# A convolution, attention and expert kernel: norms, roots and routing of its last part by other operations, in a written-out order

## The chip, the cores and the metric

The kernel runs on one core of a Trainium2 chip, as one launch. Its time is device time in microseconds (us), the median of several runs. A core has five engines that run side by side, each with its own queue of instructions in a fixed order: TensorE (PE in the profile, with its weight loads as PEld), VectorE (DVE), ScalarE (ACT), GpSimd (POOL) and SyncE (SP), which issues most transfers. Engines wait for each other by semaphores. TensorE writes its results to PSUM, a small memory of eight banks; the other data lie in SBUF.

## The reference

The input x has 32 images of 128 channels and 64 x 64 pixels, all float32. Layer 0 is a convolution in a butterfly-transformed domain; layer 1 is attention over the channels and a layer of eight experts of which each token takes two. A token is a pixel with its 128 channels.

```python
def reference(x, ...):
    # layer 0
    x = x + _L0_conv_ref(_gn(x), L0_conv_weight, kd1, kd2, k11, k12, k21, k22)
    # layer 1, on tokens: (32, 4096, 128)
    t = _to_tokens(x)
    t = t + _L1_attn_ref(_ln_t(t), Wk, bk, Wv, bv)
    t = t + _L1_ffn_ref(_ln_t(t), router_w, router_b, expert_w, expert_b)
    return _from_tokens(t, x)

def _ln_t(v, eps=1e-5):
    m = jnp.mean(v, axis=-1, keepdims=True)
    s = jnp.var(v, axis=-1, keepdims=True)
    return (v - m) / jnp.sqrt(s + eps)

def _L1_ffn_ref(x, router_w, router_b, expert_w, expert_b):
    router_probs = jax.nn.softmax(x @ router_w + router_b, axis=-1)
    top_p, top_i = jax.lax.top_k(router_probs, 2)
    top_p = top_p / jnp.sum(top_p, axis=-1, keepdims=True)
    expert_out = jnp.einsum('bnd,edc->bnec', x, expert_w) + expert_b
    gathered = jnp.take_along_axis(expert_out, top_i[..., None], axis=2)
    return jnp.einsum('bnk,bnkc->bnc', top_p, gathered)
```

The attention forms keys and values of each image's normed tokens, multiplies them into a 128 x 128 matrix over all 4096 tokens, takes the softmax of its rows, and applies it to every token.

## The kernel before

The kernel has three parts. The first (until about 927 us) normalizes each image and transforms it forward; the second (until about 2536 us) multiplies by the transformed weights, one column of pixels after another; the last transforms back and does the whole of layer 1. The change lies in the last part alone.

The last part works image by image, with three or four images in flight. An image's tokens lie in `tk` as 32 tiles of 128 tokens x 128 channels. Its steps, with the names that the order uses for them:

- `r0` to `r7` load the image's data of the second part, `x` loads the image itself (2 MB).
- `w0` to `w7` transform back along one axis on TensorE (tile `pu`, L903) into the one buffer `cv`, and `wo` copies it out on ScalarE (L913). `h0` to `h3` transform along the other axis (tile `py`, L925), and `ho` adds the result to the image on VectorE (L933).
- `pt0` to `pt7` turn channels into tokens on TensorE (L1049), `to` copies them to `tk` (L1054), `sa` gathers norm statistics with bn_stats on VectorE (L1021).
- `va`, `pwa` and `na` make mean and inverse root of the first norm: six small operations on VectorE (L1031 to L1036), a power of -0.5 on GpSimd (L1041), two more on VectorE (L1078, L1079).
- `xg` norms four tiles at a time on ScalarE (L1089), `pg` adds their Gram matrix up (L1100), and `gs`, `pb`, `t1`, `pb2`, `sm`, `pr`, `sr`, `sn`, `pc`, `prx` turn it into the attention matrix in `prx`, a tile that also holds the router's weights.
- `pp0`, `pp3` to `pp30` multiply three tiles of tokens each by `prx` (L1173); `at` scales the product on ScalarE (L1186) and copies the router's part to `lq` (L1190); `ad` adds it to `tk` and gathers the statistics of the second norm (L1201, L1021).
- `vb`, `pwb`, `lg`, `nb` make the second norm and the logits; `l2` to `f4`, `f5` and `gt` find the two best experts of each token and their weights, on arrays of 128 x 256 (L1246 to L1276).
- `xn` norms the tokens (L1301), `px` and `xT` turn them (L1311, L1317), `pe` multiplies a tile by four experts (64 an image, L1324), `m` weighs the result on VectorE (L1335), `s` sums the eight experts of a pair of tiles on GpSimd (L1360, L1361, L1363; 16 an image), `st` turns tokens back to channels (tile `po`, L1370), `so` copies and stores them (L1376).

For the last image five of the sixteen pairs are weighed and added on VectorE in one step (L1347) and skip GpSimd.

PSUM's eight banks are shared out as three for `pe`, two for the one buffer `cv`, and three for all the transposes and products (`tl`: `pt`, `pg`, `pb`, `pc`, `pp`, `px`, `po`).

A planner sets the order. Each step is entered with its engine, an estimated length, a due time, the steps it follows, and the buffers that it takes and frees; the due time is the image's number times a slot of 114 us, with a shift for each kind of step. The planner plays the program through once with these lengths, gives each engine the due step that comes first among those that can start, and emits the instructions in the order so found. `prepare` (step `prep`, 3.5 us in the plan) folds the means over the channels into the expert, key and value weights; it comes after `h3` of the first image.

The lines on which the roots and the first sums rest:

```python
nc.vector.tensor_add(total, even[:, :, 1], odd[:, :, 1])
...
nc.vector.scalar_tensor_tensor(var, diff, 0.25, var, ALU.mult, ALU.add)
...
nc.gpsimd.tensor_tensor(rstd, var, mhalf, ALU.pow)
...
nc.vector.scalar_tensor_tensor(nmr, total, -0.5, rstd, ALU.mult, ALU.mult)
```

Of the kernel before, what the change touches and what calls it, by code (L numbers as in the profile page):

```python
# [16 lines left out]
P = 128  # L17
# [3 lines left out]
NE = 8  # L21
# [3 lines left out]
class Plan:  # L25
# [12 lines left out]
    def run(self):  # L38
# [46 lines left out]
        self.length = now  # L85
        for i in order:
            ops[i][3]()
# [3 lines left out]
def kernel(  # L91
# [702 lines left out]
    tps = pool("tps", 3, space=PSUM)  # L794
# [26 lines left out]
    rws = kc.tile([P, NE], F32, name="rws")  # L821
# [7 lines left out]
    def prepare():  # L829
# [21 lines left out]
        nc.vector.tensor_scalar_mul(rws, pe[:, 0:NE], float(P))  # L851

    plan = Plan({"cv": 1, "pe": 3, "tl": 3, "r": 10, "x": 2, "xg": NG, "xn": 2, "xT": 2, "tm": 2, "so": 2, "gate": 2})
    SLOT = 114.0

    SHIFT = {
        "ad": -0.15, "at": -0.25, "f": 0.71, "gs": -1.97, "gt": 0.71, "h": -0.24, "ho": -3.5, "kvp": 3.43,
        "kvq": -0.45, "l": 0.71, "lg": 3.61, "m": -0.32, "na": -1.87, "nb": -0.81, "pb": -1.97, "pc": -1.97,
        "pe": 0.16, "pg": -0.08, "pp": 0.19, "pr": -1.97, "prx": -1.97, "pt": -0.23, "pwa": -1.87, "pwb": 3.61,
        "px": 0.15, "r": -0.04, "s": 0.08, "sa": 1.29, "sm": -1.97, "sn": -1.97, "so": 2.13, "sr": -1.97,  # L860
        "st": 1.1, "t": -1.97, "to": 0.06, "va": -1.87, "vb": 3.61, "w": 0.28, "x": -0.68, "xT": -0.68,
        "xg": 0.21, "xn": 2.42,
    }
    made = {}

    def add(b, key, engine, us, at, run, after=(), take=(), free=(), late=0.0):


        names = [k if isinstance(k, tuple) else (b, k) for k in after]
        at += SHIFT.get(key.rstrip("0123456789_"), 0.0)  # L870
        made[b, key] = plan.add(
            engine, us, SLOT * at, run, [made[k] for k in names if k[0] >= 0], take, free, late
        )


    def transfers(b):
# [4 lines left out]
        def load_r(e):  # L881
            def run():
                i = 8 * b + e
                ring, tag = (rp, "r") if i % 10 < 8 else (rp2, "r2")
                t = rs[b, e] = ring.tile([P, 16 * n], F32, tag=tag, name=f"r{b}_{e}")
                for r in range(2):
                    nc.sync.dma_start(t[r * n : (r + 1) * n], pfv[b, e, r])
            return run
# [6 lines left out]
        add(b, "x", "SP", 0.1, b + 0.2, load_x if b else (lambda: None), take=("x",), late=12.0 if b else 0.0)  # L895

    def conv(b):
        def w_inverse(e):

            def run():  # L900
                ps = tile_of["cv", b, e] = cps.tile([P, 8, P], F32, tag="cv", name=f"pu{b}_{e}")
                for k in range(8):
# [3 lines left out]
                    )  # L906
            return run
# [31 lines left out]
        def w_inverse_piece(e, oh):  # L939

            def run():
                ps = tile_of["cw", b, e, oh] = eps.tile([P, 8, n], F32, tag="pe", name=f"pw{b}_{e}_{oh}")
                for k in range(8):
                    lo = (2 * k + oh) * n
                    for r in range(2):
                        nc.tensor.matmul(
                            ps[r * n : (r + 1) * n, k, :], rs[b, e][:, lo : lo + n], qw[:, r, :], start=True, stop=True
                        )
            return run
# [28 lines left out]
        if b < 2:  # L978
            for e in range(8):
                at = b + 0.08 * e  # L980
                for oh in range(2):
                    add(
                        b, f"w{e}_{oh}", "PE", 0.95, at + 0.04 * oh, w_inverse_piece(e, oh),
                        [f"r{e}"] + [(b - 1, f"h{k}") for k in range(4)], ("pe",), ("r",) if oh else (),
# [13 lines left out]
            if b == 0:  # L998
                add(b, "prep", "PE", 3.5, 0.98, prepare, ["h3"], ("pe",), ("pe",))
# [14 lines left out]
    def front(b):  # L1014
# [4 lines left out]
        def bn(bs, lo, hi):  # L1019
            for i in range(lo, hi):  # L1020
                nc.vector.bn_stats(bs[:, i].rearrange("p a s -> p (a s)"), t[:, i, :])  # L1021

        def moments(which):

            bs = v["bs"]
            even, odd = bs[:, :, 0, :], bs[:, :, 1, :]
            m2 = st.tile([P, 6, NT], F32, name=f"m2{which}_{b}", tag=f"m2{which}", bufs=2)
            total, diff, var, nmr, rstd, above = (m2[:, k, :] for k in range(6))
            if which == 1:
                v["above"] = above  # L1030
            nc.vector.tensor_add(total, even[:, :, 1], odd[:, :, 1])  # L1031
            nc.vector.tensor_sub(diff, even[:, :, 1], odd[:, :, 1])
            nc.vector.tensor_add(var, even[:, :, 2], odd[:, :, 2])
            nc.vector.tensor_mul(diff, diff, diff)
            nc.vector.tensor_scalar(var, var, 1.0 / P, LN_EPS, ALU.mult, ALU.add)
            nc.vector.scalar_tensor_tensor(var, diff, 0.25, var, ALU.mult, ALU.add)  # L1036
            v[which] = total, var, nmr, rstd

        def power(which):
            total, var, nmr, rstd = v[which]  # L1040
            nc.gpsimd.tensor_tensor(rstd, var, mhalf, ALU.pow)  # L1041
# [17 lines left out]
        def stats1(g):  # L1059
            def run():  # L1060
                if g == 0:
                    v["bs"] = st.tile([P, NT, 2, 3], F32, name=f"bs1_{b}", tag="bs", bufs=2)
                bn(v["bs"], 4 * g, 4 * g + 4)
# [9 lines left out]
        add(b, "va", "DVE", 1.7, s1 + 0.14, lambda: moments(1), [f"sa{g}" for g in range(8)])  # L1073
        add(b, "pwa", "POOL", 5.5, s1 + 0.14, lambda: power(1), ["va"])

        def nmr1():
            total, var, nmr, rstd = v[1]
            nc.vector.scalar_tensor_tensor(nmr, total, -0.5, rstd, ALU.mult, ALU.mult)  # L1078
            nc.vector.tensor_scalar_add(v["above"], nmr, 1.0)  # L1079

        add(b, "na", "DVE", 0.9, s1 + 0.14, nmr1, ["pwa"])


        def norm(g):
            def run():
                total, var, nmr, rstd = v[1]
                for k in range(4):
                    i = 4 * g + k
                    nc.scalar.activation(  # L1089
                        xg[g % NG][:, k, :], t[:, i, :], AF.Identity, bias=v["above"][:, i : i + 1], scale=rstd[:, i : i + 1]  # L1090
# [65 lines left out]
        add(b, "pb", "PE", 0.35, at, kv1, ["gs"], ("tl",))  # L1156
# [21 lines left out]
        def scaled(lo, m):  # L1178
            def run():
                total, var, nmr, rstd = v[1]  # L1180
                ps = tile_of["pp", b, lo]
                if lo == 0:
                    v["lq"] = st.tile([P, NT, 2, NE], F32, name=f"lq{b}", tag="lq")
                for k in range(m):
# [4 lines left out]
                    )  # L1189
                nc.scalar.copy(  # L1190
                    v["lq"][:, lo : lo + m].rearrange("p k r e -> p k (r e)"),
                    ps[:, 0 : m * QX].rearrange("p (k q) -> p k q", q=QX)[:, :, P:QX],
# [3 lines left out]
        def added(lo, m):  # L1196
            def run():
                if lo == 0:
                    v["bs"] = st.tile([P, NT, 2, 3], F32, name=f"bs2_{b}", tag="bs", bufs=2)
                ps = tile_of.pop(("pp", b, lo))[:, 0 : m * QX].rearrange("p (k q) -> p k q", q=QX)  # L1200
                nc.vector.tensor_tensor(t[:, lo : lo + m, :], ps[:, :, 0:P], t[:, lo : lo + m, :], ALU.add)  # L1201
                bn(v["bs"], lo, lo + m)
            return run

        for j, lo in enumerate(range(0, NT, 3)):
            m = min(3, NT - lo)
            at = s1 + 0.45 + 0.016 * j
            add(b, f"pp{lo}", "PE", 0.26 * m, at, product(lo, m), ["prx", (b - 1, "lg")], ("tl",), ("x",) if lo == 30 else ())
# [6 lines left out]
                [f"at{lo}"] + (["ad0"] if lo else [f"pg{g}" for g in range(8)]), (), ("tl",),  # L1215
# [12 lines left out]
        def logits1():  # L1228
            total, var, nmr, rstd = v[1]
            lg, eq, lq = row("lg"), row("eq"), v["lq"]  # L1230
            v["lg"], v["eq"] = lg, eq
            nc.vector.scalar_tensor_tensor(nmr, v[2][0], -0.5, nmr, ALU.mult, ALU.add)
            nc.vector.tensor_tensor(lg, lq[:, :, 0, :], by_expert(rstd), ALU.mult)
            nc.vector.tensor_add(lg, lg, lq[:, :, 1, :])
            nc.vector.tensor_tensor(eq, by_expert(nmr), by_token(rws), ALU.mult)
            nc.vector.tensor_add(lg, lg, eq)

        def nmr2():
            total, var, nmr, rstd = v[2]
            nc.vector.scalar_tensor_tensor(nmr, total, -0.5, rstd, ALU.mult, ALU.mult)  # L1240
            nc.vector.tensor_scalar_add(nmr, nmr, 1.0)
            tile_of["norm", b] = rstd, nmr

        def first_max(k):
            m, f, oh = v["tops"][:, 2 * k, :], v["tops"][:, 2 * k + 1, :], v["oh"][k]
# [223 lines left out]
```

## Time and profile before

| what | value |
| --- | --- |
| median of 3 runs | 6045.02 us (6044.08 to 6048.14) |
| the profiled execution | 6034.45 us, its span 6032.7 us |
| granted TensorE clock over the span | 0.994 |
| last part | from about 2536 us to the end |
| one image in the middle of the last part | 106.37 us |

The profile is that of one execution. It gives each instruction's engine, line, tile and duration; a group row gives the number of such instructions, their summed time on the engine, the mean length of one in ns, and how long the engine stood idle just before them and what ended that. Instructions of one engine that overlap are counted once in the busy time, so a row's busy time can be below the mean times the count. Two rows of the last part on engines other than TensorE, as examples:

```profile
L1041 POOL TENSOR_TENSOR m<-m,mhalf 128x32 f32<-128x32 f32 x63 | 342.9, 5442 | 102.7 <-DVE m L1036 102.7
L1248 DVE TENSOR_TENSOR eq<-eq,rank 128x256 f32<-128x256 f32 x64 | 84.8, 1325 | 2.2
```

The first is the power of both norms, two an image; the second one of the steps of the top-2 search.

### The profile page before, as it was taken

What the parts mean: (1) busy time and instruction counts of PE and PEld (TensorE: products, weight loads), DVE (VectorE), ACT (ScalarE), POOL (GpSimd) and SP (SyncE); (2) the same over time, 40 slices, a digit from 0 to 9 for tenths busy, and PEclk for the clock granted to TensorE, in tenths of its full rate; (3) what the DMA queues carried; (4) which work ended last, traced back from release to release, by engine and by line L of the source; (5) the groups of instructions that cost most, each with busy time, mean ns of one, the idle gap of its engine ahead of it and who ended that gap; (6) DMA issues with size and microseconds to landing.
All of it is one profiled execution on the core that took longest, in us unless ns stands there. A gap on an engine that the chain in (4) does not pass through costs nothing.

```text
span 6032.7 us, 219314 instructions
## 1 busy us (share of the span) xinstructions
PE 5884.8 (98%) x95372; PEld 4672.1 (77%) x95372; DVE 4220.6 (70%) x7696; ACT 3757.1 (62%) x7057; POOL 4205.9 (70%) x3793
## 2 busy tenths in 40 slices
PE   7999999999999999989999999999999999999998
PEld 7999999999999999866666666666666666666654
DVE  5565545555555555458778787887878788787888
ACT  7666664555555555467766676676767666676663
POOL 2110006666666666538898998989899888998988
PEclk9999999999999999999999999999999999999999
DMA  5767766666666666632222122221322222132100
GB/s 198 240 226 236 236 217 192 174 172 173 171 173 173 171 173 172 171 102 88 81 71 98 57 98 71 83 86 57 106 63 91 78 74 95 57 100 70 66 27 28
DMA packets 554068, 756.74 MB, mean 125 GB/s; under 512 B 58320, under 2 KB 318928, under 8 KB 549008
## 3 DMA queue, kind: packets, MB, share of 16 engines
q1 hardware_dynamic: 550496, 733.64, 40.3%
q8 instruction: 749, 12.27, 0.9%
q0 software_dynamic: 2608, 9.06, 0.5%
q14 instruction: 215, 1.76, 0.1%
HBM read 406.79 MB, written 335.54 MB: 123 GB/s over the span
## 4 chain that ended last, share of the span: by engine, by line
PE 88%; ACT 7%; issue 2%; DVE 1%; POOL 1%; DMA 1%; SPq 0%; POOLq 0%; ACTq 0%; DVEq 0%
PE pe L1324 28%; PE m L658 17%; PE g L636 9%; PE pf L418 7%; PE pu L903 6%; PE pp L1173 4%; PE py L925 4%; PE pg L1100 4%; PE pv L396 3%; PE px L1311 2%; ACT xn L1301 2%; ACT u L913 2%; PE pz L373 1%; ACT z L383 1%; PE pt L1049 1%
## 5 line engine op out<-in xcount | busy, mean ns | idle before, releaser
L1324 PE MATMUL pe<-ew_sb,xT 128*128 128x512 f32 x4096 | 1946.1, 597 | 19.4 <-DVE tm L1335 16.0
L1335 DVE TENSOR_TENSOR tm<-pe,oh 128x512 f32<-128x512 f32 x2028 | 1346.4, 684 | 479.3 <-PE pe L1324 455.5
L1360 POOL TENSOR_TENSOR tm<-tm 128x512 f32<-128x512 f32 x1014 | 1286.1, 1284 | 201.1 <-DVE tm L1335 182.7
L1324 PEld LDWEIGHTS pe<-ew_sb,xT 128*128 128x128 f32 x4096 | 700.9, 191 | 522.9 <-issue 396.1
L647 DVE COPY f<-g 128x1024 f32<-128x1024 f32 x508 | 622.2, 1225 | 648.9 <-PE g L636 648.9
L658 PE MATMUL m<-f,s 128*64 128x64 f32 x32768 | 1070.1, 224 | 1.9 <-issue 1.1
L658 PEld LDWEIGHTS m<-f,s 128*64 128x64 f32 x32768 | 1000.0, 138 | 63.2 <-issue 2.6
L604 POOL COPY s<-l 128x512 f32<-128x512 f32 x512 | 546.0, 1099 | 524.9 <-issue 508.3
L647 ACT COPY f<-g 128x1024 f32<-128x1024 f32 x508 | 514.5, 1013 | 561.0 <-PE g L636 534.8
L1363 POOL TENSOR_TENSOR tk<-tk,tm 128x256 f32<-128x256 f32 x1014 | 753.6, 743 | 79.5
L1361 POOL TENSOR_TENSOR tm<-tm 128x512 f32<-128x512 f32 x507 | 650.4, 1283 | 39.8
L913 ACT COPY u<-pu 64x512 f32<-64x512 f32 x960 | 556.6, 580 | 135.1 <-PE pu L903 121.5
L636 PE MATMUL g<-c,wst 9*128 9x128 f32 x16256 | 599.9, 283 | 3.6 <-issue 3.3
L636 PEld LDWEIGHTS g<-c,wst 9*128 9x128 f32 x16256 | 502.8, 186 | 38.5 <-issue 3.9
L349 POOL TENSOR_TENSOR grstd<-gms,mhalf 128x1 f32<-128x1 f32 x32 | 17.8, 555 | 735.8 <-DVE gms L345 735.8
L1186 ACT ACTIVATE pp<-pp,m 128x128 f32<-128x128 f32 x1024 | 440.9, 431 | 124.1 <-PE pp L1173 99.3
L606 POOL TENSOR_SCALAR s<-l 128x512 f32<-128x512 f32 x256 | 509.5, 1990 | 0.0
L903 PEld LDWEIGHTS pu<-qw,r 128*128 128x128 f32 x3840 | 455.7, 193 | 63.3 <-ACT u L913 49.5
L903 PE MATMUL pu<-qw,r 128*128 128x128 f32 x3840 | 476.3, 278 | 25.6 <-ACT u L913 25.6
L1317 ACT COPY xT<-px 128x512 f32<-128x512 f32 x256 | 150.2, 587 | 560.5 <-PE px L1311 557.5
L418 PE MATMUL pf<-ph,v 128*128 128x128 f32 x4096 | 491.0, 278 | 5.0 <-ACT z L383 1.1
L418 PEld LDWEIGHTS pf<-ph,v 128*128 128x128 f32 x4096 | 466.9, 192 | 14.7 <-ACT z L383 7.1
(177 smaller groups left out, 8573.0 us busy)
## 6 DMA issues: line engine op xcount, KB each, us to landing
xf<-f SPq DMA_DIRECT2D x512, 256.0 KB
pf<-o SPq DMA_DIRECT2D x1016, 128.0 KB
l<-xf SPq DMA_DIRECT2D x1012, 128.0 KB
r<-pf SPq DMA_DIRECT2D x496, 256.0 KB
x<-in_x_dram SPq DMA_DIRECT2D x256, 256.0 KB
out_dram<-so SPq DMA_DIRECT2D x256, 256.0 KB
y<-in_x_dram SPq DMA_DIRECT2D x31, 2048.0 KB
r<-pf POOLq DMA_DIRECT2D x16, 248.0 KB, 7.7
```

The source lines that it names most:

```text
L418: nc.tensor.matmul(pl[:, j * P : (j + 1) * P], vs[b][:, 8 * g + j, :], ph.rearrange("h r m -> h (r m)"), start=True, stop=True,)
L604: nc.gpsimd.tensor_copy(dst, src)
L636: nc.tensor.matmul(pg[g // 2][:, g % 2, m * P : (m + 1) * P], wst[rows, 16 * half + 4 * t + m, :], c[rows].rearrange("r h k -> r (h k)"), ...
L647: copy(f.rearrange("i m (g o) -> i m g o", g=2), tile_of["g", w, half, t][k].rearrange("i g (o m) -> i m g o", o=4))
L658: nc.tensor.matmul(ps[hh * n : (hh + 1) * n, q, :], s[:, h].rearrange("i k b -> i (k b)")[:, B * r : B * r + n], f[:, h, r, :], start=(r = ...
L903: nc.tensor.matmul(ps[:, k, :], rs[b, e][:, k * P : (k + 1) * P], qw.rearrange("w r m -> w (r m)"), start=True, stop=True,)
L913: nc.scalar.copy(u[r * n : (r + 1) * n, :, oh * n + 8 * e : oh * n + 8 * e + 8], ps[oh * n : (oh + 1) * n, :, r * n : (r + 1) * n].rearran ...
L1324: nc.tensor.matmul(ps, tile_of["xT", b, i // 4][:, i % 4, :], ew_sb[:, es, :].rearrange("d e c -> d (e c)"), start=True, stop=True,)
L1335: nc.vector.tensor_tensor(tile_of["tm", b, i // 2][:, i % 2, es, :], tile_of.pop(("pe", b, i, half)).rearrange("p (e c) -> p e c", c=P), t ...
L1360: nc.gpsimd.tensor_tensor(tm[:, k, 0:4, :], tm[:, k, 0:4, :], tm[:, k, 4:8, :], ALU.add)
L1361: nc.gpsimd.tensor_tensor(tm[:, :, 0:2, :], tm[:, :, 0:2, :], tm[:, :, 2:4, :], ALU.add)
L1363: nc.gpsimd.tensor_tensor(t[:, lo : lo + 2, :], t[:, lo : lo + 2, :], tm[:, :, m, :], ALU.add)
```

## The change

Seven things are changed, all in the last part.

1. bn_stats is followed by bn_aggr for each tile, which gives mean and variance; the six small operations on VectorE are gone.
2. The inverse root is an exponential of a logarithm on ScalarE (`power`), followed by a Newton step on GpSimd (`newton`), where the shifts are made too.
3. The router's weights are centred once, in `prepare`; the logits are built in PSUM while the product is still there, one small VectorE operation a tile, and only half of `lq` is copied.
4. The arrays `lg` and `eq` of the top-2 search lie in PSUM (tile `sc`), so that every step of it has at most one operand in SBUF. One addition moves to ScalarE.
5. For that, the transposes and products have two PSUM banks instead of three.
6. The store is a step of its own (`os`) on SyncE, and the buffers of the loads are taken in the order in which they were freed.
7. The planner no longer finds the order. `follow` emits the steps in a list written out for one image's length: each entry names a step and the stage, so that `pe8_0:4` at turn p is that of image p - 4. The first two and the last two images have small offsets for each kind of step. `prepare` comes beside `pwa` of the first image.

```diff
-    tps = pool("tps", 3, space=PSUM)
+    tps = pool("tps", 2, space=PSUM)
+    sc = pool("sps", 1, space=PSUM).tile([P, 2, NT, NE], F32, name="sc")
...
-        nc.vector.tensor_scalar_mul(rws, pe[:, 0:NE], float(P))
+        for t in prx:
+            nc.vector.tensor_tensor(t[:, P + NE : QX], t[:, P + NE : QX], pe[:, 0:NE], ALU.subtract)
...
+        def bn(which, lo, hi):
+            bs = st.tile([P, 4, 6], F32, name=f"bs{which}_{b}_{lo}", tag="bs", bufs=2)
             for i in range(lo, hi):
-                nc.vector.bn_stats(bs[:, i].rearrange("p a s -> p (a s)"), t[:, i, :])
+                nc.vector.bn_stats(bs[:, i - lo, :], t[:, i, :])
+            for i in range(lo, hi):
+                nc.vector.bn_aggr(v["mv", which][:, i, :], bs[:, i - lo, :])
...
+        def power(which):
+            w = v[which] = st.tile([P, 5, NT], F32, name=f"ln{which}_{b}", tag=f"ln{which}", bufs=2)
+            nc.scalar.activation(w[:, 0, :], v["mv", which][:, :, 1], AF.Ln, bias=epsc)
+            nc.scalar.activation(w[:, 0, :], w[:, 0, :], AF.Exp, scale=-0.5)
+
+        def newton(which):
+
+            mv = v["mv", which]
+            rstd, nmr, above, var, q = (v[which][:, k, :] for k in range(5))
+            nc.gpsimd.tensor_scalar_add(var, mv[:, :, 1], LN_EPS)
+            nc.gpsimd.tensor_tensor(q, var, rstd, ALU.mult)
+            nc.gpsimd.tensor_tensor(q, q, rstd, ALU.mult)
+            nc.gpsimd.tensor_scalar(q, q, -0.5, 1.5, ALU.mult, ALU.add)
+            nc.gpsimd.tensor_tensor(rstd, rstd, q, ALU.mult)
+            nc.gpsimd.tensor_tensor(nmr, mv[:, :, 0], rstd, ALU.mult)
+            nc.gpsimd.tensor_scalar(above, nmr, -1.0, 1.0, ALU.mult, ALU.add)
             if which == 1:
...
+                nc.gpsimd.tensor_scalar_mul(nmr, nmr, -1.0)
...
                 nc.vector.tensor_tensor(t[:, lo : lo + m, :], ps[:, :, 0:P], t[:, lo : lo + m, :], ALU.add)
-                bn(v["bs"], lo, lo + m)
+                for k in range(m):
+                    nc.vector.scalar_tensor_tensor(
+                        sc[:, 0, lo + k, :], ps[:, k, P : P + NE], v[1][:, 0, lo + k : lo + k + 1], v["lq", lo][:, k],
+                        ALU.mult, ALU.add,
+                    )
+                bn(2, lo, lo + m)
...
+            nc.vector.tensor_copy(first, v["tops"][:, 0, :])
+            nc.vector.tensor_tensor(v["tops"][:, 5, :], v["tops"][:, 2, :], first, ALU.subtract)
...
             nc.scalar.activation(g2, g2, AF.Exp)
+            nc.scalar.activation(g1, g2, AF.Copy, bias=1.0)
...
-            nc.vector.tensor_scalar_add(g1, g2, 1.0)
...
-    plan.run()
+    ORDER = """
+        na:3 xn5:4 xT3:4 pe8_0:4 pe9_0:4 m8_0:4 s3:4 xg0:3 m9_0:4 m8_1:4 st0:4 h1:2 xg1:3 pe9_1:4 so0:4 xg2:3 os0:4
...
+        xn7:4 s7:4 pc:3 pe16_0:4 r6:1 prx:3 xT5:4 pe16_1:4 m16_0:4 m17_1:4 pp0:3 m16_1:4 pe17_0:4 at0:3 r1:0 pp6:3
+        m17_0:4 h2:2 at6:3 ad0:3 s8:4 r4:1 ad6:3 pe18_1:4 pp9:3 ho2:2 pe19_1:4 r7:0 at9:3 pe18_0:4 st3:4 m18_0:4
+        h3:2 so3:4 m18_1:4 os1:4 ad9:3 pp3:3 ho3:2 pe19_0:4 at3:3 pp12:3 m19_0:4 pe23_1:4 m19_1:4 at12:3 ad3:3 s9:4
+        w0:1 ad12:3 pe22_0:4 r3:0 wo0_0:1 pp24:3 m22_0:4 pe22_1:4 at24:3 m23_1:4 px6:4 m22_1:4 pe20_0:4 xT6:4 ad24:3
+        pe23_0:4 wo0_1:1 pp30:3 m23_0:4 pe20_1:4 at30:3 m20_0:4 s11:4 pp21:3 ad30:3 w1:1 at21:3 m20_1:4 pp15:3
+        ad21:3 r5:0 wo1_0:1 pe21_1:4 at15:3 pe21_0:4 pe26_0:4 m21_0:4 os3:4 wo1_1:1 m21_1:4 pp18:3 ad15:3 s10:4
+        pe27_1:4 at18:3 w2:1 m26_0:4 ad18:3 pp27:3 wo2_0:1 pe26_1:4 x:1 m27_1:4 at27:3 pe27_0:4 m26_1:4 px7:4
+        m27_0:4 wo2_1:1 pe25_1:4 ad27:3 s13:4 pe24_1:4 xT7:4 pe24_0:4 pwb:3 w3:1 m24_0:4 m25_1:4 m24_1:4 pt1:2
+        pe30_0:4 to1:2 wo3_0:1 pe25_0:4 nb:3 m30_0:4 pt0:2 m25_0:4 st4:4 to0:2 pe30_1:4 s12:4 l2:3 wo3_1:1 pe31_1:4
...
+    """
...
+    plan.follow(list(dict.fromkeys(i for at, i in sorted(turns))))
```

## What the change should do to the time

> **What bounds the kernel now.** I read the page's rows of busy time and clock first, then the granted clock and busy time of one image's length in the last part, then TensorE's waits, then VectorE's rows in order of time.
>
> ```profile
> span 6032.7 us, 219314 instructions
> PE 5884.8 (98%) x95372; PEld 4672.1 (77%) x95372; DVE 4220.6 (70%) x7696; ACT 3757.1 (62%) x7057; POOL 4205.9 (70%) x3793
> ...
> PEclk9999999999999999999999999999999999999999
> ```
>
> TensorE is busy nearly throughout, at a clock that is hardly held back. The change touches only the last part, from about 2536 us on. There the kernel repeats itself: the copy of the Gram matrix (L1113) starts at 5040.77 and again at 5147.14, so one image takes 106.37 us. A stretch of that length, with the columns window, PE, PEld, DVE, ACT, POOL, clock, DMA share, GB/s:
>
> ```profile
> 4000.00:4106.00 106.00, 104.65 (x743) 71.61 (x742) 85.14 (x189) 72.87 (x167) 94.91 (x83) 1.00 0.24 80
> ```
>
> TensorE is idle 1.35% of the time, 1.43 us an image; VectorE, ScalarE and GpSimd all have room. TensorE's waits from 3000 to 5500 us (total, times, longest) say where:
>
> ```profile
> PE pt L1049 <- ACT tk L1054: 18.2, 23, 0.8
> PE pu L903 <- ACT u L913: 12.3, 23, 0.5
> ```
>
> Two places, both behind ScalarE. So in the middle some 28 images hold 28 x 1.43 = 40 us to win, however much work leaves VectorE and GpSimd. The rest lies at the ends: by busy time in stretches of 20 us, TensorE idles 28 of the 220 us from 2540 on and 34 of the last 272.
>
> **The change part by part.** Durations are those of the profiled execution.
>
> *GpSimd.* Two powers leave, each L1041 at 5.44 us. Two Newton sequences of 8 and 7 short operations come; the nearest rows are 128x1 at 0.22 (L353) and 128x64 at 0.34 (L618), so 0.22 to 0.29 each, about 3.8 us. Net 7 us an image less on an engine 95 us busy of 106. In the middle this is worth nothing: TensorE does not wait for it there.
>
> *VectorE, removed.* Moments (L1031 to L1036) 3.6, L1078/1079 0.9, L1232 to L1236 1.9, L1240/1241 1.4, L1272 1.1: 8.9 us an image. The top-2 steps cost 12.0 now because some stretch (L1248 means 1.33, while L1236 of the same shape takes 0.44); at 0.42 each the sixteen take 6.7, 5.3 less.
>
> *VectorE, added.* Aggregations, 64 an image, and 32 scalar-times-tensor steps of 128x8 that build the logits in PSUM. For the latter, L1347 (128x128) takes 350 ns and L339 (128x1) 220, so 0.225; the second and third of a group write the same tile and wait for the one before, as L1247 waits for L1246 and starts 0.04 after its end: 8 us an image. The aggregation has one row only:
>
> ```profile
> L328 DVE BATCH_NORM_AGGREGATE gmv<-gbs x32: 371/372/374, 13.9 to 840.1; 128x2 f32<-128x48 f32 x32
> ```
>
> It reads 16 triples, the new one 2. If the 0.217 us above a shortest operation (0.155) goes by triples, two take 0.03, and behind others an operation hides about 0.085 (bn_stats: 0.28 alone, 0.195 in a row). That is 0.10. Below, 0.08 is the step of short operations less their elements; above, 0.29 is the row itself less the overlap. I take 0.10, since the row's length is most simply explained by what it reads, and keep both ends. VectorE's ledger: 85.1 - 8.9 - 5.3 + 0.2 + 8.0 + 6.4 = 85.5. No relief in sum, and it is bunched: the new work sits in the pieces that free the PSUM buffers of the products. In these rows of now (start, length) a piece is an addition and three bn_stats, done 1.26 us after it began:
>
> ```profile
> 5053.37 0.56 DVE L1201 TENSOR_TENSOR tk<-pp,tk 128x384 f32<-128x384 f32 x1
> 5053.96 0.68 DVE L1021 BATCH_NORM_STATS2 bs<-tk 128x6 f32<-128x128 f32 x3
> 5054.63 1.22 DVE L933 TENSOR_TENSOR y<-py,y 128x1024 f32<-128x1024 f32 x1
> ```
>
> After: 0.49 (addition) + 0.225 + 2 x 0.26 - 0.085 + 3 x 0.195 + 3 x 0.10 = 2.03 us.
>
> *The new order and two transposing buffers instead of three.* I add up the tightest stretch, pp0 to pp30. TensorE does 6 products (0.74), 10 expert products (0.86), 2 h-inverses (2.02), one w-inverse (1.78) and 2 groups of transposes (0.44): 19.7; all of an image's operations so added give 103.6 against 104.9 busy, so 20.0. pp30 takes the buffer that ad24 frees. VectorE reaches ad0 2.5 us in (0.74, a wait of 0.17, ScalarE's 1.57) and does 6 pieces, 2 additions of h (1.14) and 7 weighings (0.60): 6 x 2.03 + 2.28 + 4.2 = 18.7. It ends at 21.3, 1.3 us too late. In general the stall is 18 x a - 0.5, with a the aggregation: 0.9 at 0.08, 1.3 at 0.10, 4.7 at 0.29. Other places in the image are earlier than that by the same sums, so one stall of 1.3 takes the place of 1.43 idle: 0.15 us an image won, 28 x 0.15 = 4 us. While the Gram matrix holds one of the two buffers, st1 and px4 share the other, 3.5 us apart at some 1.2 us of use: no stall.
>
> *ScalarE.* Root and inverse become logarithm and exponential. The page has one row for a table load, ACT_TABLE_LOAD at 1.283 us; the built program has 128 more of them, four an image: each logarithm and each exponential has its own. The Trainium skill (ScalarE: Activation LUTs, What ACT_TABLE_LOAD costs) counts 2.66 us for every switch, the load and a drain; and its section on table sets says that logarithm and exponential share a set, which would need one load where the program has two. By the row, a power is 2 x 1.283 + 2 x 0.23 = 3.0 us; by the page's price, 5.8. ScalarE goes from 73 to 79, or to 84.5. The power waits for the last product piece; queued behind it are the copies to1 and wo3, for which TensorE's st4 (buffer) and w4 wait, and on GpSimd the Newton steps nb and na stand before the sums s12 and s3. In the same frame the last piece ends at 36.2, the power at 39.3 by the row, to1 at 39.9; st4 is due at 40.7. Cover 0.7 us. By the page it is 2.0 late. I take the row, which is this chip's own; whether a drain follows, its trace cannot show, since ScalarE waits for the norm after that load. 5.8 stays as the far end.
>
> *SP.* Loads of r and x and stores stand in one fixed line now, a store waiting for ScalarE before later loads. r2 is issued 33 us before its use and took 7.7 us where the page times it; x (2 MB, at 170 GB/s about 12 us) 41 us before. Nothing, unless a store is held 25 us.
>
> *The head.* On the first image's chain moments, power and shift (1.8 + 5.44 + 0.9) become 3.0 + 2.0: 3 us. prepare (3 us of TensorE and a wait of 2.3 for VectorE behind it) moves beside that chain. I count 5 of the 28 us.
>
> *The tail.* Here GpSimd counts: it is busy 243 of the last 272 us. After the last product TensorE now has 88 expert products; in the built new order 78. Pairs for GpSimd go from 17 to 14.5 at 5.42 us: 92 + 5.4 become 79 + 2, TensorE's own work 87 becomes 76, so idle time 29.6 becomes 23, some 6 us won; a shorter top-2 chain before it (VectorE is 94% busy from 5820 to 5860) gives 3. Together 9.
>
> **Sum.** 4 + 5 + 9 = 18 us off the profiled execution's 6034.45 (span 6032.7): 6016. The median of the runs is 10.6 above it: **6027**.
>
> **Rivals.** A measurement here tells 0.2%, 12 us, from no change.
>
> *A clean order*: if the 128x8 steps cost what L851 (128x8, 0.16) does, each piece is 0.2 shorter and the stall goes. For it: 0.2 x 6 is just the 1.3. Against: L1347 and L339. 40 + 14 = 54 us: 5991.
>
> *VectorE becomes the bound (slower)*: the aggregation has a fixed cost. Place: product pieces, then the bn groups behind the transposes (32 more of them). From a = 0.14 the stall of 2.0 eats the 14 us of the ends; at 0.20 it is 3.1, 28 x 1.65 = 46, less 14: 6077; at 0.29, 6122. For it: the only row is 0.37. Against: it reads eight times as much.
>
> *The table switch costs what the page says (slower)*: 2.0 at st4 and up to 1 at the other power: 2.5, 28 x 1.07 = 30 less 14: 6061.
>
> **Chances.** Sum as worked out 0.36 (own range 6010 to 6040, a from 0.08 to 0.11 and the ends between 5 and 20 us); clean order 0.25; VectorE 0.25; table 0.14. Of the first about a third lies within 0.2%. Faster 0.50, same 0.12, slower 0.38. The range, 5985 to 6085, holds the clean order and all but the dear end of the aggregation.
>
> **What would show it.** The aggregation's mean below 0.12 in a row; a product piece of 2.0 us; one TensorE wait an image, pp on tk at about 1 us, with those on ScalarE gone; table loads with less than 0.3 us between load and next operation; GpSimd near 88 us an image. Wrong if TensorE waits over 2 us an image, if st or pu wait behind ScalarE's power, or if VectorE passes 92 us of the 105.

## The result and the profile after

The changed kernel takes 5989.18 us (5988.73 to 5990.17), the kernel before 6044.55 (6039.15 to 6048.14): 55.4 us less, a ratio of 0.9909 with a 95% interval of 0.9892 to 0.9927. The profiled execution took 5989.13 us. From its page:

```profile
span 5987.4 us, 222395 instructions
PE 5870.1 (98%) x95372; PEld 4672.1 (78%) x95372; DVE 4105.6 (69%) x10097; ACT 3975.3 (66%) x7345; POOL 3950.1 (66%) x4210
...
PE 91%; ACT 3%; DVE 2%; POOL 2%; issue 1%; DMA 0%; SPq 0%; POOLq 0%; DVEq 0%; ACTq 0%
```

The span is 45.3 us shorter. The last line is the chain that ends last, by engine: TensorE holds more of it (88% before), ScalarE less (7% before). In a stretch of one image's length, with the columns window, PE, PEld, DVE, ACT, POOL, clock, DMA share, GB/s:

```profile
4000.00:4105.00 105.00, 105.00 (x746) 72.08 (x745) 82.47 (x270) 80.34 (x178) 87.25 (x95) 1.00 0.26 81
```

TensorE shows no idle time. The list of its waits from 3000 to 5500 us has no row at all, where the kernel before had 30 us behind `pt` and `pu` (the two rows in the prediction). The copy of the Gram matrix, once an image, gives the period (first and last start in the window; before, then after):

```profile
L1113 DVE COPY gs<-pg x26: 290/292/293, 3019.7 to 5679.0; 128x128 f32<-128x128 f32 x26
```

```profile
L1121 DVE COPY gs<-pg x27: 291/291/293, 3031.9 to 5745.9; 128x128 f32<-128x128 f32 x27
```

That is 2659.3 / 25 = 106.37 and 2714.0 / 26 = 104.38 us an image: 1.99 less, though TensorE's idle time was only 1.34 an image. From image 4 to image 30 the kernel wins 51.7 us (2765.7 to 2714.0). The Gram copy of image 4 comes 12.2 us later (3019.66 and 3031.89), and from image 30 to the end the kernel wins 5.8 (247.3 to 241.5).

Most of the 12.2 us lies ahead of the last part, where nothing was changed. The matmuls of the second part (first and last start; before, then after):

```profile
L658 PE MATMUL m<-f,s x32768: 222/222/369, 941.6 to 2536.4; 128*64 128x64 f32 x200
```

```profile
L671 PE MATMUL m<-f,s x32768: 216/222/368, 944.4 to 2543.5; 128*64 128x64 f32 x200
```

The last one starts 7.1 us later; 5.1 us of that are there after three quarters of them (2136.9 and 2142.0). The profiled execution before, 6034.45 us, was quicker than each of the four that give the median. So the last part itself loses 5.1 us up to image 4 and wins 5.8 from image 30 on: its ends change the time by less than 1 us.

The new operations, in the list of groups (busy time and mean ns; idle time before them):

```profile
L1209 DVE SCALAR_TENSOR_TENSOR sc<-pp,ln,lq 128x8 f32<-128x8 f32 x1024 | 236.4, 231 | 23.9
L1033 DVE BATCH_NORM_AGGREGATE mv<-bs 128x2 f32<-128x6 f32 x2048 | 199.9, 158 | 0.0
...
L1251 DVE TENSOR_TENSOR sc<-sc,rank 128x256 f32<-128x256 f32 x64 | 27.7, 432 | 2.2
```

One aggregation's record lasts 158 ns on average, but they overlap: 199.9 / 2048 = 0.098 us of VectorE each. The top-2 step that took 1.325 us takes 0.432. The root of one norm on ScalarE, in order of time (start, length):

```profile
5058.21 1.28 ACT L1037 ACT_TABLE_LOAD   x1
5059.50 0.32 ACT L1037 ACTIVATE ln<-mv,eps 128x32 f32<-128x32 f32 x1
5059.84 1.28 ACT L1038 ACT_TABLE_LOAD   x1
5061.14 0.23 ACT L1038 ACTIVATE ln<-ln 128x32 f32<-128x32 f32 x1
```

Each load is followed by its operation within 0.02 us; the whole takes 5061.37 - 5058.21 = 3.16 us, and the next eviction starts 0.11 later.

The stall that the prediction put at `pp30` is absent. VectorE's rows of the piece `ad24`, and TensorE's rows of `pp30` (four matmuls) and `pp21` (six) beside it:

```profile
5042.13 0.55 DVE L1207 TENSOR_TENSOR tk<-pp,tk 128x384 f32<-128x384 f32 x1
5042.59 0.76 DVE L1209 SCALAR_TENSOR_TENSOR sc<-pp,ln,lq 128x8 f32<-128x8 f32 x3
5043.27 0.67 DVE L1031 BATCH_NORM_STATS2 bs<-tk 128x6 f32<-128x128 f32 x3
5043.85 0.30 DVE L1033 BATCH_NORM_AGGREGATE mv<-bs 128x2 f32<-128x6 f32 x3
```

```profile
5042.98 0.65 PE L1181 MATMUL pp<-prx,y 128*128 128x144 f32 x4
5043.47 1.02 PE L1319 MATMUL pe<-ew_sb,xT 128*128 128x512 f32 x2
5044.33 0.90 PE L1181 MATMUL pp<-prx,y 128*128 128x144 f32 x6
```

`pp30` starts 0.37 us before the last 128x8 step of `ad24` has ended (5043.35). So it cannot be using that bank; in the built program it uses the one that the eviction `xT6` freed, and `pp21` takes `ad24`'s (the runs with a bank of choice, below, test this). And the statistics, which end at 5044.15, read `tk` in SBUF: the bank is free 0.8 us before the piece is done.

### The profile page after: what moved, and what is told of

Its sections match the earlier page's. It is cut to its first block, busy times and chain, and to the rows that moved or that the text cites. A ratio compares the mean times of both kernels' runs of the same rounds, so it can differ in the third digit from the quotient of the medians.

```text
span 5987.4 us, 222395 instructions
## 1 busy us (share of the span) xinstructions
PE 5870.1 (98%) x95372; PEld 4672.1 (78%) x95372; DVE 4105.6 (69%) x10097; ACT 3975.3 (66%) x7345; POOL 3950.1 (66%) x4210
## 4 chain that ended last, share of the span: by engine, by line
PE 91%; ACT 3%; DVE 2%; POOL 2%; issue 1%; DMA 0%; SPq 0%; POOLq 0%; DVEq 0%; ACTq 0%
PE pe L1319 28%; PE m L671 17%; PE g L649 9%; PE pu L910 7%; PE pf L431 7%; PE py L933 4%; PE pp L1181 4%; PE pg L1108 4%; PE pv L409 3%; PE pt L1062 2%; PE px L1306 2%; PE po L1365 2%; PE pz L386 1%; ACT z L396 1%; POOL tm L1355 1%
## 5 line engine op out<-in xcount | busy, mean ns | idle before, releaser
L1319 PE MATMUL pe<-ew_sb,xT 128*128 128x512 f32 x4096 | 1967.4, 597 | 21.8 <-DVE tm L1330 12.6
L1330 DVE TENSOR_TENSOR tm<-pe,oh 128x512 f32<-128x512 f32 x2028 | 1322.7, 682 | 547.6 <-PE pe L1319 420.6
L1319 PEld LDWEIGHTS pe<-ew_sb,xT 128*128 128x128 f32 x4096 | 688.5, 190 | 470.6 <-issue 303.1
L1358 POOL TENSOR_TENSOR tk<-tk,tm 128x256 f32<-128x256 f32 x1014 | 738.1, 728 | 79.5
L1192 ACT ACTIVATE pp<-pp,ln 128x128 f32<-128x128 f32 x1024 | 441.6, 431 | 267.2 <-PE pp L1181 120.4
L1031 DVE BATCH_NORM_STATS2 bs<-tk 128x6 f32<-128x128 f32 x2048 | 449.7, 280 | 18.4 <-ACT tk L1067 15.1
```

Of the source, the lines that this page charges most:

```text
L1319: nc.tensor.matmul(ps, tile_of["xT", b, i // 4][:, i % 4, :], ew_sb[:, es, :].rearrange("d e c -> d (e c)"), start=True, stop=True,)
L1330: nc.vector.tensor_tensor(tile_of["tm", b, i // 2][:, i % 2, es, :], tile_of.pop(("pe", b, i, half)).rearrange("p (e c) -> p e c", c=P), t ...
L1358: nc.gpsimd.tensor_tensor(t[:, lo : lo + 2, :], t[:, lo : lo + 2, :], tm[:, :, m, :], ALU.add)
```

## The experiments

Two questions: is the gain the order's or the operations', and was the prediction's stall a wrong idea or a right one in the wrong place? All runs are of the whole kernel. "Period" is worked out from the Gram copies as above; "idle" is TensorE's idle time from 3300 to 5500 us over the images in it (2200 / period). In e1_planner the images come in pairs, so that its period is taken over 22 images.

| run | us (lowest to highest) | ratio to before, 95% | period | idle an image |
| --- | --- | --- | --- | --- |
| before (first series) | 6044.55 (6039.15 to 6048.14) | | 106.37 | 1.34 |
| after | 5989.18 (5988.73 to 5990.17) | 0.9892 to 0.9927 | 104.38 | 0.00 |
| e1_planner | 6487.15 (6482.74 to 6490.33) | 1.0719 to 1.0751 | 121.34 | 9.68 |
| e10_oldorder | 6069.24 (6068.01 to 6073.3) | 1.003 to 1.006 | 107.16 | 1.57 |
| e2_pow | 6203.22 (6196.51 to 6205.8) | 1.0249 to 1.0279 | 111.17 | 3.93 |
| e3_sbuf | 6172.19 (6169.25 to 6172.79) | 1.0198 to 1.0229 | 110.58 | 4.36 |
| e4_aggr2 | 6020.92 (6018.94 to 6023.02) | 0.995 to 0.9978 | 105.25 | 0.31 |
| e6_tables2 | 6113.37 (6109.08 to 6117.92) | 1.0102 to 1.0132 | 108.10 | 3.23 |
| e5_late | 6014.12 (6007.28 to 6020.87) | 0.9936 to 0.9966 | 105.02 | 0.01 |
| e7_same | 5987.94 (5981.19 to 5988.87) | 0.9889 to 0.9922 | 104.38 | 0.00 |
| e7_bank | 6008.83 (6003.05 to 6015.81) | 0.9928 to 0.9958 | 104.98 | 0.37 |
| e7_bank_late | 6052.72 (6049.92 to 6053.44) | 1.0005 to 1.0024 | 106.24 | 1.32 |
| e8_prep | 5986.47 (5980.69 to 5994.67) | 0.9895 to 0.9928 | 104.36 | 0.00 |
| e9_direct4 | 5991.13 (5990.29 to 5991.89) | 0.99 to 0.9929 | 104.38 | 0.00 |

### The operations without the order

First the planner again, with its former shifts and its lengths for two kinds of step:

```diff
-    plan.follow(list(dict.fromkeys(i for at, i in sorted(turns))))
+    plan.run()
```

> All new operations of the change (bn_aggr, the logarithm and exponential with the Newton steps on GpSimd, the 128x8 step, the SBUF squares, the prefetched first stage) but without the fixed order: the greedy planner places the steps, with its former shifts and planned lengths. It tells apart where the 55 us come from. Theory T (the gain is that TensorE no longer waits for ScalarE at the evictions, which is the order's work): the waits behind pt and pu stay, 6030 to 6050 us. Rival R (less work on VectorE and ScalarE is the gain, whatever the order): 6000 us or less, with under 0.5 us of TensorE waits an image.

Measured: 6487 us, far from both. TensorE's waits from 3300 to 5600 us (total, times, longest) begin:

```profile
PE pp L1190 <- DVE sc L1218: 52.5, 44, 2.6
PE pu L919 <- ACT u L930: 23.8, 34, 1.7
PE pp L1190 <- ACT pp L1201: 16.3, 19, 1.0
```

The products wait for VectorE's 128x8 steps. This shows that the planner with shifts made for the old steps places the new ones badly, not what they are worth. So the second form: the new operations in the very step order that the kernel before ran, handed over as a list.

```diff
-    tps = pool("tps", 2, space=PSUM)
-    sc = pool("sps", 1, space=PSUM).tile([P, 2, NT, NE], F32, name="sc")
+    tps = pool("tps", 3, space=PSUM)
+    sc = kc.tile([P, 2, NT, NE], F32, name="sc")
...
-    plan.follow(list(dict.fromkeys(i for at, i in sorted(turns))))
+    plan.follow([made[int(b), k] for b, k in words])
```

> The new operations in the step order that the kernel before ran, step by step (the logarithm and exponential where the moments stood, the Newton steps where the power stood, each store after its eviction). The scratch of scores stands in SBUF, since the old order needs three PSUM banks in the tail. It is the fair form of the question that the planner run left open, since the planner placed the new steps with shifts that fit the old ones. Theory T (operations and order belong together: ScalarE's 6.3 us an image of logarithms and exponentials fall among the evictions that TensorE waited for): 6030 to 6080 us. Rival R (the operations are worth something by themselves): 6015 us or less.

Measured: 6069.24, some 25 us slower than before. TensorE's waits from 3300 to 5500 us are those of the kernel before, and one more:

```profile
PE pt L1062 <- ACT tk L1067: 16.7, 21, 0.8
PE pu L910 <- ACT u L921: 11.2, 21, 0.5
PE pe L1319 <- DVE tm L1330: 3.7, 20, 0.2
```

The time is theory T's, rival R falls: in the old order the two places behind ScalarE stay (16.7 and 11.2 us; 16.6 and 10.7 before, in the same stretch), whatever VectorE and GpSimd have shed (VectorE 1737 against 1762 us busy in these 2200, GpSimd 1810 against 1970). That the logarithms among the evictions cost the 25 us, as theory T has it, is not shown: these two waits hardly grew. The scratch in SBUF leaves one part of the change out; in PSUM it wouldn't fit, since the old order needs three banks in the tail.

### The order without one of the operations

The power back on GpSimd, in place of logarithm, exponential and Newton steps:

```diff
-            nc.scalar.activation(w[:, 0, :], v["mv", which][:, :, 1], AF.Ln, bias=epsc)
-            nc.scalar.activation(w[:, 0, :], w[:, 0, :], AF.Exp, scale=-0.5)
...
+            nc.gpsimd.tensor_tensor(rstd, var, mhalf, ALU.pow)
```

> The fixed order kept, but the root taken again as a power with a half on GpSimd, in one instruction for each norm: no logarithm, no exponential, no table loads on ScalarE, no Newton steps. GpSimd gets some 8 to 9 us an image more (87 to about 96 of 104.4), ScalarE 6.3 less, VectorE as before. Theory T (the order is fitted to what the steps cost, and a step that grows on any engine brings waits back): 0.5 to 2 us an image, 6005 to 6050 us. Rival R (GpSimd has the room, the roots could have stayed): 5985 to 5995 us.

Measured: 6203 us, beyond both. ScalarE, then TensorE in order of time, with the idle time before a row in brackets:

```profile
4002.22 1.65 ACT L1291 ACTIVATE xn<-tk,ln 128x128 f32<-128x128 f32 x4 [3.18 <-POOL ln L1045]
4003.90 0.58 ACT L1062 COPY tk<-pt 128x512 f32<-128x512 f32 x1
```

```profile
4004.53 0.66 PE L1057 MATMUL pt<-ident,y 128*128 128x128 f32 x4 [2.07 <-ACT tk L1062]
4048.37 0.44 PE L1360 MATMUL po<-ident,tk 128*128 128x128 f32 x2 [1.61 <-POOL tk L1353]
```

The power lasts 5.46 us and the root comes late. `xn0` stands waiting for it at the head of ScalarE's queue; the eviction behind it, which needs no root, is late too, and TensorE waits 2.07 us for its bank. On GpSimd the power delays the sums of pairs in the same way (the second row). GpSimd is 86% busy from 3300 to 5500 us: room in the sum is of no use to a queue whose head is late.

The scratch back in SBUF:

```diff
-    sc = pool("sps", 1, space=PSUM).tile([P, 2, NT, NE], F32, name="sc")
+    sc = kc.tile([P, 2, NT, NE], F32, name="sc")
```

> The fixed order kept, but the scratch of scores and masks (lg, eq) in SBUF instead of PSUM, as before the change; nothing else moves. The top-2 steps go back from about 0.43 us to the 0.8 to 1.3 us that they took beside GpSimd's own work, about 5 us an image more on VectorE (80 to 85 of 104.4). Theory T: the late gates shift the last products and bring waits back, 0.1 to 1 us an image, 5995 to 6020 us. Rival R (VectorE has 24 us of room in a period, the late steps cost nothing): 5986 to 5992 us.

Measured: 6172 us, 183 us more than the changed kernel where theory T allowed 31. The top-2 step at L1251 takes 1.10 us again. Among all waits from 4000 to 4600 us, the exponential in the middle of the top-2 search, first in the changed kernel and then with SBUF:

```profile
ACT tops L1265 <- DVE tops L1261: 6.8, 6, 1.1
```

```profile
ACT tops L1265 <- DVE tops L1261: 25.8, 5, 5.2
```

1.1 us each became 5.2. Behind the exponential ScalarE has the eviction `xT` in its queue, and TensorE's `po` waits for that bank; expert products wait for the weighings of a later VectorE:

```profile
4094.48 1.12 PE L1319 MATMUL pe<-ew_sb,xT 128*128 128x512 f32 x2 [0.81 <-DVE tm L1330]
4100.40 0.66 PE L1365 MATMUL po<-ident,tk 128*128 128x128 f32 x4 [2.58 <-ACT xT L1312]
```

From 3300 to 5500 us the two places sum to this:

```profile
PE po L1365 <- ACT xT L1312: 51.5, 20, 2.6
PE pe L1319 <- DVE tm L1330: 33.6, 36, 1.9
```

The expectations took VectorE at 80 us of a period and ScalarE at 76; the profile of the changed kernel has 82 and 80.

### The disputed costs, doubled

Every aggregation twice:

```diff
             for i in range(lo, hi):
                 nc.vector.bn_aggr(v["mv", which][:, i, :], bs[:, i - lo, :])
+            for i in range(lo, hi):
+                nc.vector.bn_aggr(v["mv", which][:, i, :], bs[:, i - lo, :])
```

> The fixed order kept, every bn_aggr done twice: 64 more of them an image, 6.3 us of VectorE (80.3 to 86.6 of 104.4), spread in pieces of 0.3 us over the statistics steps. If VectorE's pieces really set the product buffers free late, as the sum in the prediction had it (1.3 us at pp30 with 0.05 of cover), the wait grows and the time is 6020 to 6040 us. If the buffer is free after the 128x8 step and 0.9 us of slack lie behind it, as the timeline of the changed kernel reads: 5989 to 6000 us. If VectorE's load counts at all and not its place: some 3 us an image, 6070 us.

Measured: 6020.92, at the foot of the first case's figures, but not by its mechanism. There is one wait an image, and it is not at a product but at an expert product whose bank VectorE frees by a weighing behind the longer pieces (3300 to 5600 us):

```profile
PE pe L1321 <- DVE tm L1332: 6.3, 22, 0.3
```

VectorE is busy 4232.9 us instead of 4105.6, thus 4.0 us more an image and not 6.3, since the second aggregations overlap too; the period grows by 0.87. In the prediction's sum this is an aggregation of 0.098 + 0.062 = 0.16 and a stall of 18 x 0.16 - 0.5 = 2.4 us an image. So its rival "VectorE becomes the bound" had the right direction, but neither the place nor the price.

The logarithm and exponential twice:

```diff
             nc.scalar.activation(w[:, 0, :], w[:, 0, :], AF.Exp, scale=-0.5)
+            nc.scalar.activation(w[:, 0, :], v["mv", which][:, :, 1], AF.Ln, bias=epsc)
+            nc.scalar.activation(w[:, 0, :], w[:, 0, :], AF.Exp, scale=-0.5)
```

> The fixed order kept, the pair of logarithm and exponential done twice for each norm: two more table loads and two more small steps, 3.1 us more of ScalarE each time, 6.3 an image (76 to about 83 of 104.4); the root then has another value, its time alone is looked at. It shows what the roots on ScalarE would have cost if a switch of tables cost about twice what the profile has. After the runs with the power and with the scratch in SBUF, where 3 to 4 us of lateness at a waiting place cost about 6 us an image, theory T: 2 to 6 us an image, 6045 to 6165 us. Rival R (ScalarE stands idle for 28 us in a period, the loads hide): 5988 to 5998 us.

Measured: 6113 us, theory T. The two waits an image, from 3300 to 5500 us:

```profile
PE po L1367 <- ACT tk L1069: 33.8, 21, 1.6
PE po L1367 <- POOL tk L1360: 31.8, 20, 1.6
```

The first is the place that the prediction named: `st4` behind `to1` behind the power, with 3.1 - 1.6 = some 1.5 us of cover where it had 0.7. At the second, TensorE waits for GpSimd's sums, which stand behind the Newton steps of the first norm, late at the head of its queue.

### The stall at pp30

First the end of the piece. The three 128x8 steps, the last readers of the bank, go behind the statistics:

```diff
+                bn(2, lo, lo + m)
                 for k in range(m):
                     nc.vector.scalar_tensor_tensor(
...
-                bn(2, lo, lo + m)
```

> In each product piece the three 128x8 steps, the last readers of the product's PSUM bank, stand behind the statistics instead of ahead of them: same instructions, the bank is held until the end of the piece, as the prediction's sum had it, some 0.9 us later than in the changed kernel. If the product that takes the bank next has the 0.9 us of slack that the timeline of the changed kernel reads (pp21 after ad24): 5987 to 6000 us, no wait behind the 128x8 steps. If the end of the piece decides, as the prediction had it: a wait of about 1.2 us an image at a product, 6020 us or more.

Measured: 6014 us, between the two. TensorE shows no idle time, and still the period is 0.64 us longer. Two rows of the weight loads, from 3300 to 5500 us, are not in the changed kernel's list:

```profile
PEld pp L1181 <- DVE sc L1210: 20.7, 42, 0.7
PEld px L1306 <- ACT pp L1192: 15.8, 21, 1.1
```

A product is preceded by the load of its weights. The first load and the matmuls of `pp21`, in the changed kernel and here:

```profile
5043.90 0.19 PEld L1181 LDWEIGHTS pp<-prx,y 128*128 128x128 f32 x1 [0.24 <-DVE bs L1031]
5044.33 0.90 PE L1181 MATMUL pp<-prx,y 128*128 128x144 f32 x6
```

```profile
5066.22 0.79 PEld L1181 LDWEIGHTS pp<-prx,y 128*128 128x128 f32 x6 [0.75 <-DVE sc L1210]
5066.22 1.00 PE L1181 MATMUL pp<-prx,y 128*128 128x144 f32 x6
```

In the changed kernel the load runs 0.43 us ahead of its matmul, beside the matmuls before; here it is held until 0.05 us after the last 128x8 step and starts with its matmul. Laid beside each other by the starts of their matmuls over one image, the two kernels drift apart in one stretch of 7 us only, from a `px` over three products to the step behind the last, by some 0.1 us at each: this is the whole 0.64. So 0.9 us of slack, read from matmul to matmul, was too much. That the lost overlap of the loads is the cause is read from these rows and not tested by itself; VectorE is also 1.0 us an image busier here (4137.4 against 4105.6).

Then the bank. A control hands the two banks out by an explicit list; in `e7_bank` only `pp30` takes the last of the free ones, which is `ad24`'s; `e7_bank_late` moves the 128x8 steps as well.

```diff
 # control
-                ps = tile_of["pp", b, lo] = tps.tile([P, 512], F32, tag="tl", name=f"pp{b}_{lo}")
+                ps = tile_of["pp", b, lo] = tl_take(f"pp{b}_{lo}")
 # e7_bank
-                ps = tile_of["pp", b, lo] = tl_take(f"pp{b}_{lo}")
+                ps = tile_of["pp", b, lo] = tl_take(f"pp{b}_{lo}", lo == 30)
```

> Control for the next two: the two PSUM banks of the tail are handed out by an explicit list, first freed first taken, instead of by the pool. The products sit in the same banks as in the changed kernel; some transposes of the experts change banks. Both theories: 5985 to 5995 us.

> As the control, but the product pp30 takes the bank that ad24 frees last, which the prediction assumed, instead of the one that the eviction xT6 has freed before. Theory T (only the choice of the bank took the predicted stall away): pp30 waits 0.4 to 0.5 us for the last 128x8 step of ad24, with the lost overlap 0.6 to 1 us an image, 15 to 30 us over the control. Rival R (a wait so short is taken up by work elsewhere in the period): within 5 us of the control.

> Both faults of the prediction's sum put into the kernel: pp30 takes the bank that ad24 frees, and the 128x8 steps stand at the end of the piece. Theory T: pp30 waits 1.2 to 1.4 us an image, as the prediction had it, 40 to 55 us over the control, thus 6030 to 6045 us. Rival R (VectorE, being then late in no other place, makes good for it within the period): under 20 us over the control.

Measured: 5987.94 for the control; with the bank 6008.83, 21 us more; with both faults 6052.72, 65 more. `pp30` in the two kernels:

```profile
4949.09 0.73 PE L1193 MATMUL pp<-prx,y 128*128 128x144 f32 x4 [0.36 <-ACT u L929]
```

```profile
4984.36 0.74 DVE L1222 SCALAR_TENSOR_TENSOR sc<-pp,ln,lq 128x8 f32<-128x8 f32 x3
...
4985.25 0.73 PE L1193 MATMUL pp<-prx,y 128*128 128x144 f32 x4 [1.36 <-DVE sc L1222]
```

With the bank that the prediction assumed and the piece freeing it at its end, `pp30` waits 1.36 us, right behind the last 128x8 step. The prediction had 1.3. Theory T holds in its mechanism; its 40 to 55 us were too few. The 65 us also hold the loss of the late steps by themselves, 0.64 us a period in the run before.

The first row names ScalarE's copy `u`, which is no input of `pp30`. It ended at 4949.00, VectorE's last 128x8 step of `ad24` at 4948.94: the profile names the later of two that ended close together. The weight load of `pp30` starts at 4949.06, 0.12 us after VectorE's step, and in the second kernel 0.12 us after it too (4985.22 and 4985.10). That the bank is the cause follows from the control, which has no such wait.

### The ends

```diff
-            add(b, "prep", "PE", 3.5, 1.2, prepare, [f"sa{g}" for g in range(8)], ("pe",), ("pe",))
+            add(b, "prep", "PE", 3.5, 1.2, prepare, ["h3"], ("pe",), ("pe",))
```

The step's place in the list moves with it.

> The fixed order kept, but the preparation of the centred router at its former place, behind h3 of the first image instead of behind its norm statistics. The head of the changed kernel is 12 us longer than before, with some 2.5 us of exposed waits in the preparation. If its new place costs: 3 to 8 us faster, 5981 to 5986 us. If the head's length comes from the order's fill: 5987 to 5992 us.

Measured: 5986.47, from 5980.69 to 5994.67, which can't be told from the changed kernel. In the profiled execution the Gram copy of image 4 came at 3024.5 instead of 3031.9, but 2.8 of these 7.4 us were there at the last matmul of the second part (2540.7 and 2543.5), and other executions of the same kernel were up to 14 us longer. Of the head's 12 us, 7.1 lie ahead of the last part; what the other 5 are made of stays open.

```diff
-        direct = (3, 6, 9, 12, 15) if b == B - 1 else ()
+        direct = (4, 8, 12, 15) if b == B - 1 else ()
```

> Only the last image: four pairs of tiles (4, 8, 12, 15) weighed directly on VectorE instead of five (3, 6, 9, 12, 15). TensorE waits 7.6 us for the direct steps of VectorE in the tail, and 11.7 for its ordinary ones. If VectorE bounds the tail: 2 to 8 us faster, 5981 to 5987 us. If GpSimd does (it is at 36 of 40 us in one stretch): 2 to 5 us slower.

Measured: 5991.13, 2 us slower. The ranges lie 0.1 us apart, little beside the 14 us between runs of the kernel before this one, so neither case is shown. None of the twelve kernels is clearly better than the changed one.

## Why the prediction was off

The result, 5989, lies 4 us inside the lower end of the range (5985 to 6085), not in the likeliest case (6010 to 6040), and the gain is three times the 18 us that the sum gave. It is at the time of the rival "a clean order" (5991), but that agreement is luck: the 128x8 steps are not cheap (0.231 us), and the rival's 40 + 14 us were 51.7 in the middle and about nothing at the ends.

**What held.** Aggregation 0.098 in a row (0.10); 128x8 step 0.231 (0.225); product piece `ad24`, from 5042.13 to 5044.15, 2.02 us (2.03); the root on ScalarE 3.16 (3.0); top-2 steps 0.43 (0.42); GpSimd 87 us an image (88); VectorE 82.5 (85.5), ScalarE 80.3 (79). On the table switch the row was right and the price of the Trainium skill (ScalarE: Activation LUTs, What ACT_TABLE_LOAD costs), 2.66 us with its drain, was not seen: the operation behind a load starts within 0.02 us. The run with two pairs shows that the choice mattered, since 3.1 us more on each power cost 124 us.

**The step that failed** is "pp30 takes the buffer that ad24 frees", with the buffer free when the piece is done: "It ends at 21.3, 1.3 us too late." Two faults lie in it. The pool here hands out the bank freed first in the order of the program, which is `xT6`'s. And a bank is free with its last reader, the third 128x8 step, not with the statistics, which read SBUF. Put both into the kernel, and the predicted stall is there, at its place and size (1.36 for 1.3). Put in the bank alone: 0.36. The late step alone: no idle time, 0.64 us lost. Neither: none. The rest of the sum was sound, but for a slip: 2.5 + 18.7 is 21.2 and not 21.3, a stall of 1.2.

**The price of a stall was mis-sized.** "28 x 1.43 = 40 us to win" takes idle time for lost time. The 1.43 is itself too high: the line shown has 1.35 us of 106, which is 1.27%, and from 3300 to 5500 us it is 1.34 an image. The experiments give, over the period of 104.38: 0.37 idle, 0.60 lost (`e7_bank`); 1.32 and 1.86 (`e7_bank_late`); 0.31 and 0.87 (`e4_aggr2`); 0.01 and 0.64 (`e5_late`). On top of the idle time come 0.2 to 0.6 us, most likely the overlap that the next weight load loses. In the same way an image without the 1.34 us of idle time of before is 1.99 us shorter, and the 26 images measured 51.7.

**The ends gave nothing.** "I count 5 of the 28 us" for the head and "Together 9" for the tail. Measured in equal windows from the last matmul of the second part on, TensorE idles 32.7 us instead of 31.5 in 464 us, and 36.3 instead of 34.4 in the last 228. In the tail GpSimd did get lighter (183 us busy instead of 200), and TensorE's waits for its sums fell from 7.4 to 4.0, those for VectorE's ordinary weighings from 16.0 to 11.7. But waits for the direct weighings grew from 2.4 to 7.6, and products now wait 5.3 us, which did not wait before. That the tail is 5.8 us shorter all the same goes with the place of `gs30` in the order: 164 expert products are left behind it and not 171, 7 x 0.86 = 6.0 us of work that now lies ahead of it. In sum: predicted -4 in the middle and -14 at the ends, measured -51.7 and -0.7, beside 7.1 us by which these two executions differ ahead of the last part.

**Where the gain comes from.** Not from the operations alone (in the old order, with the scratch in SBUF: slower than before), and not from the order alone, which turns slower than before without the root on ScalarE or without the scratch in PSUM. The two belong together: with these operations in this order TensorE does not wait in the middle, and each of the two that were taken back brings waits. The new order with all the old operations was not run. That VectorE gets "no relief in sum" was 3 us off (82.5 for 85.5) and beside the point, since no wait hung on its sum.

## What to carry to other kernels

In a fixed order with in-order queues, ask of each step what stands behind it, not how much room its engine has: where an exponential came 4 us later on ScalarE, an eviction queued behind it held TensorE for 2.6 us of the 4.4 that it stood idle in each image. Before summing towards a PSUM bank, find which bank it is and who reads it last; those two facts made 65 us here. And read the weight loads' waits beside the matmuls': a TensorE with no idle time can still lose 0.6 us in every period.

## What the runs showed that was not expected

A wait can cost twice. In the run with the scratch in SBUF, in windows of 3 us (columns as above), around the wait of 2.58 us that ends at 4100.40:

```profile
4098.00:4101.00 3.00, 0.59 (x5) 0.60 (x6) 2.96 (x13) 1.68 (x5) 0.87 (x2) 1.00 0.00 0
4101.00:4104.00 3.00, 3.00 (x6) 1.29 (x5) 2.96 (x6) 2.91 (x6) 2.47 (x2) 0.62 0.23 87
4104.00:4107.00 3.00, 3.00 (x13) 1.52 (x11) 2.83 (x4) 1.71 (x5) 2.76 (x4) 0.81 0.61 169
```

The granted clock falls to 0.62 and 0.81 in the 6 us after. With TensorE busy throughout, I estimate 3 x 0.38 + 3 x 0.19 = 1.7 us lost on top of the wait. This does not follow every wait. From 3300 to 5500 us, over the 6 us after a wait, the clock was between 0.72 and 0.75 after 13 of the 20 waits of 2.6 us in this run and 1.00 after the other seven. In the run with the power it was 0.72 after 12 of 20 waits of 2.1 us and after 11 of 20 of 1.6 us, and 1.00 after the rest. One of those eleven, the wait of 1.61 us that ends at 3489.22:

```profile
3486.22:3489.22 3.00, 1.32 (x8) 0.80 (x7) 0.02 (x1) 3.00 (x8) 2.77 (x4) 1.00 0.23 87
3489.22:3492.22 3.00, 3.00 (x10) 1.99 (x11) 1.96 (x3) 3.00 (x9) 2.92 (x3) 0.57 0.00 0
```

In the run with two pairs of tables it stayed at 1.00 after all 41 waits of 1.6 us. So the length of the wait alone does not decide it, and what does stays open. The Trainium skill (TensorE: Matmul & The Clock Gate, The HAM clock gate) has the clock halved after an idle window of about 3.4 us; here waits of 1.6 to 2.6 us were enough at times. By these counts the slower clock costs 23/20 x 1.7 = 2.0 us an image with the power and 13/20 x 1.7 = 1.1 with the scratch in SBUF. This is part of why these two runs passed every expectation: 3.9 and 4.4 us idle an image became 6.8 and 6.2 lost.
